# A one-core kernel of three nested Strassen levels: third level for three more pairs of steps, and the first loads on two queues

## The chip, the cores and the metric

The kernel runs on one core of one Trainium2 chip. The metric is the device time of one execution in microseconds. The core has the engines TensorE (PE, with its weight loads shown apart as PEld), VectorE (DVE), ScalarE (ACT), GpSimd (POOL) and SyncE (SP). SP computes nothing here; it issues most of the DMAs, and ACT and POOL issue the rest, each in the order of its own program.

## The reference

Two layers with residuals, all in f32, on x of 32 x 128 x 2048:

```python
x = x + ffn0(cond0(x))      # layer 0
x = x + ffn1(cond1(x))      # layer 1

# cond0: a mixture of 8 kernels of 128 x 128, weighted by an attention of the condition
att = softmax(gelu(gelu(emb @ W0 + b0) @ W1 + b1) @ W2 + b2)
out = einsum('boi,bih->boh', einsum('bk,koi->boi', att, weight), x) + (att @ bias_k)[:, :, None]

# ffn0: a dense layer 2048 -> 2048 with 16 low-rank updates of rank 16 (A, Bf)
out = einsum('bsd,od->bso', x, W) + bias
upd = einsum('ebsr,eor,e->bso', einsum('bsd,erd->ebsr', x, A), Bf, coeffs * scales)

# cond1: a grouped convolution of 9 taps along the 2048 (4 groups), plus ctx(cond) + bias
# ffn1: columns permuted, 16 heads of 128 -> 512 -> gelu -> 512 -> 128, columns permuted back
```

The kernel folds the low-rank updates into W (W plus scaled A times B^T), multiplies x by that W first, and applies the mixture afterwards, since both are linear.

## The kernel before, in words

**The large product.** x times W is a 2 x 2 block product by Strassen's scheme with seven products, in Winograd's form with its shared sums, at two levels. The outer level gives the seven rounds P1, P2, P6, P7, P5, P3, P4 (in this order). A round has eight steps g = 0 to 7, one for each group of four batch rows, so there are 56 steps. Each step is an inner scheme of seven products of 128 x 512 matmuls, four of them per product (`multiply`, line 342 for the DVE additions and L349 for the matmuls). f32 matmuls appear twice in the trace, so a step has 56 of them.

**The third level.** Where `in_pair(r, g)` holds, the steps g and g + 1 form a pair (`multiply_third`). Inner products P2 and P4 are left out of both steps (L439 shows the other five), and the pair makes them together in the odd step by a third scheme of seven quarter products of half-width matmuls (L450, additions L458). It needs `sq`, four sums over the pair's x tiles (`third_inputs`, L417 to L420, on POOL, but on DVE in round P6 and for g = 0), and two tiles of quarter weights (`third_weights`, L393 to L396 on POOL for the first, four operations on DVE, L1108, for the second). The partial results of the even step (`olds`) are held until the odd step has ended, and both are stored then (L277). `THIRD` names the rounds, and `SKIP` three pairs that are taken out.

**What surrounds a step.** SP loads the next step's x (L268) and the partial results (L273). POOL makes x's outer sums (L283) and inner sums (L311 to L314) in `x_combine`. At steps 2 to 6 the next round's outer weights are loaded (L507) and combined (L283), and at the end of a round `inner_weights` makes their inner sums (L252 to L256). DVE also makes the mixed kernels of `cond0` (L546) in steps 1 to 6 of most rounds.

**Slots.** All large tiles, of 8 KB per partition, share one pool of `SLOTS` = 25. A tile that is written first by a load or an operation waits in its engine's queue until a slot has been given back. Nothing behind it on that queue goes past it. The order of the instructions is the order of the source (`manual_schedule`), so it is written by hand throughout.

**The start.** After two warm-up matmuls on zeros (L157), A and B^T are loaded in pieces, A is scaled with `wsc` (L145), and for the first four W blocks `w_make` multiplies A by B^T (L180) and adds W (L184). W comes by L164. The other twelve blocks are made two at a time by a Strassen scheme (`w_make_two`, L223 and L226) ahead of the steps of round P1. Its sums of B^T (L211) are made between the additions of the fourth W block.

**The small chain.** `small()` computes the attention, the context of the convolution, the row indices and the convolution's weights. It is a generator, advanced once after each of the first six steps and twice after later ones, so a `yield` puts what follows behind another step's work.

**The last round and the rest.** In round P4 the kernel mixes (`mix_*`, L567 to L589) and convolves (`conv_*`) beside the steps, in stages of a third of a step. The permuted FFN (L818, L829, gathers L802, results L836) follows and takes the last 1100 us or so. `between(j)` is called after product j of a step and holds what is interleaved there.

Of the kernel before, what the change touches and what calls it, by code (L numbers as in the profile page):

```python
# [11 lines left out]
ALU = mybir.AluOpType  # L12
# [7 lines left out]
QW = 512  # L20
# [28 lines left out]


THIRD = ("P2", "P6", "P7", "P5", "P3")
SKIP = (("P2", 3), ("P6", 3), ("P5", 3))


@with_exitstack
def adaln_ffn_kernel(
# [16 lines left out]
    nc = tc.nc  # L73
# [53 lines left out]
    cs = const.tile([P, 4], FP, name="cs", tag="cs")  # L127
# [3 lines left out]
    a_sb = [slot(f"a_sb{h}", (P, 2, 2, 4, P)) for h in range(2)]  # L131
    bf_sb = [slot(f"bf_sb{h}", (P, 2, 2, QW)) for h in range(2)]

    def a_load(h, k0, k1):
        for ki in range(2):
            i0 = (2 * h + ki) * QW
            nc.sync.dma_start(
                a_sb[h][:, :, ki, k0:k1].rearrange("p c k i -> p c (k i)"),
                A[:, :, i0 + k0 * P : i0 + k1 * P],
            )  # L140
# [3 lines left out]
            cols = a_sb[h][:, c, :, k0:k1]  # L144
            nc.vector.tensor_scalar(cols, cols, wsc[:, c : c + 1], None, ALU.mult)  # L145

    def b_load(h, q, o0=0, n=QW):
        i0 = (2 * h + q) * QW + o0
        nc.sync.dma_start(bf_sb[h][:, :, q, o0 : o0 + n], BfT[:, :, i0 : i0 + n])

    def warm_up():

# [9 lines left out]
    def w_load(kh, oh, kc):  # L162
        t = slot(f"w_{kh}{oh}{kc}", (P, 2, 2, QW))
        nc.sync.dma_start(t.rearrange("p k o c -> p (k o c)"), WT[kh, oh, kc])  # L164
        return t
# [100 lines left out]
    def x_load(g, tp, kh):  # L266
        t = slot(f"xt_{g}{tp}{kh}", (P, 2, 2, QW))
        nc.sync.dma_start(t.rearrange("p k s c -> p (k s c)"), xT[g, tp, kh])  # L268
        return t
# [110 lines left out]
    def third_weights(name, rhs):  # L380


        ops, quarters = [], []
        for i, k in enumerate(("P2", "P4")):
            t = slot(f"{name}_q{i}", (P, 4, 2, NQ))
            q = {"P1": [], "P2": [], "P3": [], "P4": [], "P5": [], "P6": [], "P7": []}
            for kc in range(2):
                (r11, r12), (r21, r22) = (halves(rhs[k][2 * h + kc]) for h in range(2))
                for n, r in zip(q, (r11, r21, r22, t[:, 3, kc], t[:, 0, kc], t[:, 1, kc], t[:, 2, kc])):
                    q[n].append(r)  # L390
                if i == 0:
                    tt = nc.gpsimd.tensor_tensor
                    tt(t[:, 0, kc], r12, r11, ALU.subtract)  # L393
                    tt(t[:, 1, kc], r22, t[:, 0, kc], ALU.subtract)
                    tt(t[:, 2, kc], r22, r12, ALU.subtract)
                    tt(t[:, 3, kc], r21, t[:, 1, kc], ALU.subtract)  # L396
            quarters.append(q)
        (r11, r12), (r21, r22) = (
            [rhs["t4"][:, 2 * h : 2 * h + 2, n * NQ : (n + 1) * NQ] for n in range(2)]
            for h in range(2)  # L400
        )
        ops = [
            (t[:, 0], r12, r11), (t[:, 1], r22, t[:, 0]), (t[:, 2], r22, r12), (t[:, 3], r21, t[:, 1])
        ]
        return quarters, ops
# [452 lines left out]
    def small():  # L858
# [53 lines left out]
        for k in range(1, KEXP):  # L912
            nc.vector.scalar_tensor_tensor(
                aggb, ab[:, :, k], bk[:, k : k + 1], aggb, ALU.mult, ALU.add
            )

        for r in range(GR):
            p4 = bank()
            nc.tensor.matmul(
                p4[:, :B], lhsT=cw[:, r * P : (r + 1) * P], rhs=cond_s, start=True, stop=True  # L920
            )
            nc.vector.tensor_scalar(ctxb[:, r], p4[:, :B], fb[:, r : r + 1], None, ALU.add)
            done(p4)
        nc.vector.tensor_scalar(ctx34, ctxb, 0.75, None, ALU.mult)

        nc.vector.tensor_scalar(row, pos, 3, 9, ALU.bitwise_and, ALU.logical_shift_left)
        nc.vector.tensor_scalar(
# [62 lines left out]
    blocks = [  # L990
        (kh, oh, kc) for kh, oh in ((0, 0), (0, 1), (1, 1), (1, 0)) for kc in range(4)
    ]
    steps = [(r, g) for r in ROUNDS for g in range(NG)]
    warm_up()
    nc.sync.dma_start(cs, coeffs)
    nc.vector.tensor_tensor(wsc, cs[:, 0:2], cs[:, 2:4], ALU.mult)
    a_load(0, 0, 1)
    a_scale(0, 0, 1)
    b_load(0, 0, 0, QW // 2)
    b_load(0, 0, QW // 2, QW // 2)  # L1000
    b_load(0, 1)
    a_load(0, 1, 4)
    a_scale(0, 1, 4)
    wt = {k: w_load(*k) for k in blocks[0:2]}
    xs = {0: [x_load(0, 0, 0)]}
    for k in blocks[2:4]:
        wt[k] = w_load(*k)
    for q in range(2):
        b_load(1, q)
    for k in blocks[4:6]:  # L1010
        wt[k] = w_load(*k)
    nc.gpsimd.memset(wsum, 0.0)
# [26 lines left out]
    def olds_load(i):  # L1039
        r, g = steps[i]  # L1040
        olds[i] = [old and part_load(old, g) for old, _ in ADDED[r]]

    for i, (r, g) in enumerate(steps):
        ri = i // NG
        last_round = ri + 1 == len(ROUNDS)
        if i + 1 < len(steps):
            if i + 1 not in xs:
                xs[i + 1] = x_loads(*steps[i + 1])
            if not last_round:
                lhs[i + 1] = x_combine(*steps[i + 1], xs.pop(i + 1))  # L1050
                if r in THIRD and g == 0:
                    quarters, quarter_ops = third_weights(r, rhs)
# [42 lines left out]
        k0 = 3 * (g - NG)  # L1095
# [3 lines left out]
        def between(j):  # L1099
# [18 lines left out]
            if last_round:  # L1118
                if j == 3 and i + 1 < len(steps):
                    lhs[i + 1] = x_combine(*steps[i + 1], xs.pop(i + 1))  # L1120
                    olds_load(i + 1)
                if j in (2, 4):
                    stage(k0 + j // 2, stage_first)
                if j % 2:
                    stage_third(k0 + j // 2)
                else:
                    stage(k0 + j // 2, stage_second)
# [23 lines left out]
    for k, (g, h) in enumerate(heads):  # L1151
# [5 lines left out]
        t = ts.pop(k)  # L1157
# [75 lines left out]
```

## Time and profile before

| | us |
|---|---|
| median of 3 runs (lowest to highest) | 2597.11 (2597.05 to 2597.59) |
| the profiled execution | 2597.05 |
| its span in the profile | 2595.3 |
| PE busy in it | 2582.3 (99%) |
| POOL busy | 1321.1 (51%) |
| DVE busy | 1474.6 (57%) |
| ACT busy | 532.9 (21%) |

All times in what follows are microseconds from the start of the span. A line of the timeline gives the start and the length of a group of like instructions, the engine, the source line, the operation, the tile written <- the tiles read, the shape, the count, and in brackets the idle time of that engine just before and what ended it. A line of the windows gives the stretch, its length, and for PE, PEld, DVE, ACT and POOL the busy time and the number of instructions, then PE's granted clock, the DMA share and GB/s. An engine with q, as SPq, is the queue that issues DMAs. From 7.00 us to 36.00 us and from 1500 to 2580 us PE is busy in every window.

### The profile page before, as it was taken

The page shows a single profiled execution, that of the slowest core. Times are in us where ns is not written, and L with a number is a line of the kernel's source. Part 1 is how long each engine was busy: PE and PEld are TensorE (multiplying, and loading weights), DVE is VectorE, ACT ScalarE, POOL GpSimd, SP SyncE. Part 2 cuts the span into 40 slices and gives each one's busy share as a digit, 9 for nine tenths or more (in the row PEclk, how much of TensorE's full clock was granted, in tenths as well). Part 3 has the DMA queues.
Part 4 walks back from the last instruction along what each step waited for, and adds up shares of the span by engine and source line. Part 5 has one row for each costly group of instructions (what it writes and reads, how often), then busy time and mean ns, then how long its engine had stood idle before and what let it go on. Part 6 is the DMA issues. An engine that isn't in the chain of part 4 may idle for free. (4 is left out here: it accounts for less than half of the span.)

```text
span 2595.3 us, 21368 instructions
## 1 busy us (share of the span) xinstructions
PE 2582.3 (99%) x6876; PEld 1306.1 (50%) x6876; DVE 1474.6 (57%) x2326; ACT 532.9 (21%) x1099; POOL 1321.1 (51%) x1092
## 2 busy tenths in 40 slices
PE   9999999999999999999999999999999999999999
PEld 4444455455455555555444544555545554555543
DVE  5554465366455676554276666666666666666601
ACT  0000000000000000000011244444344444444432
POOL 7321657888976854967323234343444334434222
PEclk9999999999999999999999999999999999999999
DMA  7542458778457477474768788877777877787532
GB/s 311 221 161 98 185 194 335 303 310 331 192 227 303 178 315 300 195 308 167 246 213 267 229 301 266 257 231 228 228 231 240 257 225 223 230 257 229 163 128 89
DMA packets 188160, 608.28 MB, mean 234 GB/s; under 512 B 17680, under 2 KB 92944, under 8 KB 144016
## 3 DMA queue, kind: packets, MB, share of 16 engines
q1 hardware_dynamic: 149936, 473.74, 50.9%
q0 software_dynamic: 32704, 130.04, 14.9%
q10 hardware_dynamic: 5408, 3.13, 0.4%
q8 instruction: 55, 0.90, 0.1%
q14 instruction: 57, 0.47, 0.1%
HBM read 372.45 MB, written 200.84 MB: 221 GB/s over the span
## 5 line engine op out<-in xcount | busy, mean ns | idle before, releaser
L818 PE MATMUL bank<-t,ws 128*128 128x512 f32 x1024 | 460.3, 592 | 0.0
L829 PE MATMUL bank<-gl,ws 128*128 128x512 f32 x1024 | 460.2, 592 | 0.0
L836 POOL DMA_INDIRECT out<-t,orow x128 | 151.6, 1185 | 547.0 <-DVE t L834 480.4
L821 ACT ACTIVATE gl<-bank 128x512 f32<-128x512 f32 x512 | 306.3, 598 | 432.7 <-PE bank L818 426.3
L829 PEld LDWEIGHTS bank<-gl,ws 128*128 128x128 f32 x1024 | 194.6, 190 | 233.0 <-issue 231.5
L818 PEld LDWEIGHTS bank<-t,ws 128*128 128x128 f32 x1024 | 194.6, 190 | 226.6 <-issue 223.9
L567 POOL TENSOR_TENSOR x<-x,fb 128x512 f32<-128x512 f32 x128 | 173.1, 1381 | 213.1 <-DMA x<-in_x 126.4
L834 DVE TENSOR_TENSOR t<-bank,t 128x512 f32<-128x512 f32 x128 | 88.5, 691 | 327.1 <-PE bank L829 317.0
L573 ACT ACTIVATE bank<-w,aggb 128x512 f32<-128x512 f32 x128 | 80.9, 684 | 870.9 <-DMA w<-w_d 853.5
L439 PE MATMUL bank<-P_t,s_P 128*128 128x512 f32 x544 | 241.8, 592 | 0.0
L435 DVE TENSOR_TENSOR u<-bank,u 128x512 f32<-128x512 f32 x168 | 110.7, 688 | 194.9 <-PE bank L439 180.7
L283 POOL TENSOR_TENSOR xt<-xt,xt 128x512 f32<-128x512 f32 x128 | 162.7, 1303 | 104.9 <-DMA xt<-in_xT 97.1
L311 POOL TENSOR_TENSOR s_P<-xt 128x512 f32<-128x512 f32 x56 | 74.3, 1326 | 252.0 <-DMA xt<-in_xT 207.4
L439 PE MATMUL bank<-wo_P,s_P 128*128 128x512 f32 x448 | 199.1, 592 | 0.0
L546 DVE SCALAR_TENSOR_TENSOR ags<-mix,att_bc,ags 128x128 f32<-128x128 f32 x224 | 186.8, 834 | 4.7
L802 POOL DMA_INDIRECT t<-hx_d,row x128 | 131.6, 1028 | 61.7 <-issue 25.5
L439 PEld LDWEIGHTS bank<-P_t,s_P 128*128 128x128 f32 x544 | 103.4, 190 | 115.6 <-issue 112.6
L349 PE MATMUL bank<-P_t,s_P 128*128 128x512 f32 x352 | 154.7, 592 | 0.0
L439 PEld LDWEIGHTS bank<-wo_P,s_P 128*128 128x128 f32 x448 | 85.1, 190 | 95.2 <-issue 91.8
L674 PE MATMUL bank<-va,tw_l 128*128 128x256 f32 x512 | 121.2, 379 | 0.3 <-DVE va L658 0.3
L342 DVE TENSOR_TENSOR u<-bank,u 128x512 f32<-128x512 f32 x84 | 56.3, 685 | 112.7 <-PE bank L349 112.4
L674 PEld LDWEIGHTS bank<-va,tw_l 128*128 128x128 f32 x512 | 97.1, 190 | 41.2 <-issue 31.0
(188 smaller groups left out, 3589.9 us busy)
## 6 DMA issues: line engine op xcount, KB each, us to landing
xt<-in_xT SPq DMA_DIRECT2D x88, 1024.0 KB
u<-u_d SPq DMA_DIRECT2D x40, 1024.0 KB
wo_P<-wb_d SPq DMA_DIRECT2D x36, 1024.0 KB
u<-c_d SPq DMA_DIRECT2D x64, 512.0 KB
x<-in_x SPq DMA_DIRECT2D x32, 1024.0 KB
xg<-x SPq DMA_DIRECT2D x256, 128.0 KB
hx_d<-x1t SPq DMA_DIRECT2D x32, 1024.0 KB
hx_d<-ht SPq DMA_DIRECT2D x32, 1024.0 KB
```

The lines of the kernel that those rows point to most:

```text
L283: nc.gpsimd.tensor_tensor(out[:, i, j], a[:, i, j], b[:, i, j], op)
L349: nc.tensor.matmul(ps, lhsT=lhs[k][:, bass.ts(kc, P)], rhs=rhs[k][kc], start=first and kc == 0, stop=last and kc == 3, skip_group_check=True,)
L435: nc.vector.tensor_tensor(acc[:, si, oi], ps, acc[:, si, oi], ALU.add)
L439: nc.tensor.matmul(ps, lhsT=lhs[k][:, bass.ts(kc, P)], rhs=rhs[k][kc], start=first and kc == 0, stop=last and kc == 3, skip_group_check=True,)
L546: nc.vector.scalar_tensor_tensor(ag, mix[:, k], att, ag, ALU.mult, ALU.add)
L567: nc.gpsimd.tensor_tensor(xt[:, f], xt[:, f], late["fb"][:, f], ALU.add)
L674: nc.tensor.matmul(out, lhsT=w[:, 2 * i + r], rhs=rhs, start=first and r == 0, stop=last and r == 1, skip_group_check=True,)
L802: nc.gpsimd.indirect_dma_start(out=t.rearrange("p k t -> p (k t)"), out_offset=None, in_=hx_d[g].rearrange("l k t -> l (k t)"), in_offset= ...
L818: nc.tensor.matmul(pu, lhsT=w[:, m * P : (m + 1) * P], rhs=t[:, 0], start=True, stop=True)
L821: nc.scalar.activation(gl[m], pu, AF.Gelu)
L829: nc.tensor.matmul(pd, lhsT=w[:, (MC + m) * P : (MC + m + 1) * P], rhs=gl[m], start=(m == 0), stop=(m == MC - 1),)
L836: nc.gpsimd.indirect_dma_start(out=out, out_offset=bass.IndirectOffsetOnAxis(ap=orow[:, g, h : h + 1], axis=0), in_=t[:, 1], in_offset=None,)
```

## The change

- `SKIP` becomes empty: the last pairs (g = 6 and 7) of rounds P2, P6 and P5 run at the third level too.
- `third_weights`: for the first quarter tile, the operations that write parts 2 and 3 (L395, L396) are issued after those that write parts 0 and 1 (L393, L394) of both blocks.
- The first loads: `coeffs`, the second part of A's first block, the second half of B^T's first part and the rest of A go to ACT's queue. The rest stays on SP's.
- B^T's other half (`b_load(1, q)`) is issued ahead of W's third block, and the first x after W's third block.
- `small()` has two more `yield`s, around the context products.
- In the last round the x of step i + 2 is loaded after product 4 of step i, where it was loaded at the top of step i + 1.

```diff
--- before.py
+++ after.py
@@ -49,7 +49,7 @@
 
 
 THIRD = ("P2", "P6", "P7", "P5", "P3")
-SKIP = (("P2", 3), ("P6", 3), ("P5", 3))
+SKIP = ()
 
 
 @with_exitstack
@@ -131,10 +131,10 @@
     a_sb = [slot(f"a_sb{h}", (P, 2, 2, 4, P)) for h in range(2)]
     bf_sb = [slot(f"bf_sb{h}", (P, 2, 2, QW)) for h in range(2)]
 
-    def a_load(h, k0, k1):
-        for ki in range(2):
+    def a_load(h, k0, k1, engs=(nc.sync, nc.sync)):
+        for ki, eng in enumerate(engs):
             i0 = (2 * h + ki) * QW
-            nc.sync.dma_start(
+            eng.dma_start(
                 a_sb[h][:, :, ki, k0:k1].rearrange("p c k i -> p c (k i)"),
                 A[:, :, i0 + k0 * P : i0 + k1 * P],
             )
@@ -144,9 +144,9 @@
             cols = a_sb[h][:, c, :, k0:k1]
             nc.vector.tensor_scalar(cols, cols, wsc[:, c : c + 1], None, ALU.mult)
 
-    def b_load(h, q, o0=0, n=QW):
+    def b_load(h, q, o0=0, n=QW, eng=nc.sync):
         i0 = (2 * h + q) * QW + o0
-        nc.sync.dma_start(bf_sb[h][:, :, q, o0 : o0 + n], BfT[:, :, i0 : i0 + n])
+        eng.dma_start(bf_sb[h][:, :, q, o0 : o0 + n], BfT[:, :, i0 : i0 + n])
 
     def warm_up():
 
@@ -380,7 +380,7 @@
     def third_weights(name, rhs):
 
 
-        ops, quarters = [], []
+        others, quarters = [], []
         for i, k in enumerate(("P2", "P4")):
             t = slot(f"{name}_q{i}", (P, 4, 2, NQ))
             q = {"P1": [], "P2": [], "P3": [], "P4": [], "P5": [], "P6": [], "P7": []}
@@ -392,9 +392,11 @@
                     tt = nc.gpsimd.tensor_tensor
                     tt(t[:, 0, kc], r12, r11, ALU.subtract)
                     tt(t[:, 1, kc], r22, t[:, 0, kc], ALU.subtract)
-                    tt(t[:, 2, kc], r22, r12, ALU.subtract)
-                    tt(t[:, 3, kc], r21, t[:, 1, kc], ALU.subtract)
+                    others.append((t[:, 2, kc], r22, r12))
+                    others.append((t[:, 3, kc], r21, t[:, 1, kc]))
             quarters.append(q)
+        for op in others:
+            nc.gpsimd.tensor_tensor(*op, ALU.subtract)
         (r11, r12), (r21, r22) = (
             [rhs["t4"][:, 2 * h : 2 * h + 2, n * NQ : (n + 1) * NQ] for n in range(2)]
             for h in range(2)
@@ -914,6 +916,7 @@
                 aggb, ab[:, :, k], bk[:, k : k + 1], aggb, ALU.mult, ALU.add
             )
 
+        yield
         for r in range(GR):
             p4 = bank()
             nc.tensor.matmul(
@@ -922,6 +925,7 @@
             nc.vector.tensor_scalar(ctxb[:, r], p4[:, :B], fb[:, r : r + 1], None, ALU.add)
             done(p4)
         nc.vector.tensor_scalar(ctx34, ctxb, 0.75, None, ALU.mult)
+        yield
 
         nc.vector.tensor_scalar(row, pos, 3, 9, ALU.bitwise_and, ALU.logical_shift_left)
         nc.vector.tensor_scalar(
@@ -992,21 +996,21 @@
     ]
     steps = [(r, g) for r in ROUNDS for g in range(NG)]
     warm_up()
-    nc.sync.dma_start(cs, coeffs)
+    nc.scalar.dma_start(cs, coeffs)
     nc.vector.tensor_tensor(wsc, cs[:, 0:2], cs[:, 2:4], ALU.mult)
-    a_load(0, 0, 1)
+    a_load(0, 0, 1, (nc.sync, nc.scalar))
     a_scale(0, 0, 1)
     b_load(0, 0, 0, QW // 2)
-    b_load(0, 0, QW // 2, QW // 2)
+    b_load(0, 0, QW // 2, QW // 2, nc.scalar)
     b_load(0, 1)
-    a_load(0, 1, 4)
+    a_load(0, 1, 4, (nc.scalar, nc.scalar))
     a_scale(0, 1, 4)
     wt = {k: w_load(*k) for k in blocks[0:2]}
-    xs = {0: [x_load(0, 0, 0)]}
-    for k in blocks[2:4]:
-        wt[k] = w_load(*k)
     for q in range(2):
         b_load(1, q)
+    wt[blocks[2]] = w_load(*blocks[2])
+    xs = {0: [x_load(0, 0, 0)]}
+    wt[blocks[3]] = w_load(*blocks[3])
     for k in blocks[4:6]:
         wt[k] = w_load(*k)
     nc.gpsimd.memset(wsum, 0.0)
@@ -1119,6 +1123,8 @@
                 if j == 3 and i + 1 < len(steps):
                     lhs[i + 1] = x_combine(*steps[i + 1], xs.pop(i + 1))
                     olds_load(i + 1)
+                if j == 4 and i + 2 < len(steps):
+                    xs[i + 2] = x_loads(*steps[i + 2])
                 if j in (2, 4):
                     stage(k0 + j // 2, stage_first)
                 if j % 2:
```

## The prediction

> **What bounds the kernel now.** I read the page's busy shares first, then what TensorE (PE) waits for, then windows cut at the starts of steps, then the timeline of the engines that feed PE.
>
> ```profile
> span 2595.3 us, 21368 instructions
> PE 2582.3 (99%) x6876; PEld 1306.1 (50%) x6876; DVE 1474.6 (57%) x2326; ACT 532.9 (21%) x1099; POOL 1321.1 (51%) x1092
> ```
>
> PE is idle for 2595.3 - 2582.3 = 13.0 us. About 6 of them are the tail (from 2580 us on it is busy 9.03 of 15.3 us), which the change leaves alone. So time can come only from fewer PE instructions, or from these waits (total, times, longest):
>
> ```profile
> PE bank L223 <- DVE w L226: 2.4, 3, 1.7
> PE bank L157 <- DVE warm L154: 1.5, 1, 1.5
> PE bank L180 <- DMA bf_sb<-in_BfT: 1.0, 1, 1.0
> PE bank L349 <- DVE u L342: 0.9, 1, 0.9
> ```
>
> Next, windows of one pair of steps each (length, then busy time and instructions by engine): P2's third pair, P2's last, P7's last, P5's last.
>
> ```profile
> 399.25:445.67 46.42, 46.42 (x138) 25.84 (x137) 25.78 (x35) 0.00 (x0) 39.27 (x33) 1.00 0.82 331
> 445.67:493.73 48.06, 48.06 (x113) 21.28 (x112) 12.65 (x23) 0.00 (x0) 31.99 (x28) 1.00 0.68 264
> 820.32:866.74 46.42, 46.42 (x138) 25.84 (x136) 16.84 (x27) 0.00 (x0) 27.65 (x23) 1.00 0.53 205
> 1006.65:1054.72 48.07, 48.07 (x114) 21.28 (x113) 21.61 (x38) 0.00 (x0) 26.14 (x21) 1.00 0.65 256
> ```
>
> A third-level pair takes 46.42 us (136 weight loads, 56 of them for half-width matmuls), an ordinary one 48.06 (112 full ones), PE busy throughout in both. P7's last pair already has the third level and a full 25-slot pool around it, and PE does not wait.
>
> **Third level for three more pairs.** PE: 48.06 - 46.42 = 1.64 us each, 3 x 1.64 = **4.92 us**, if nothing new is late. What it adds elsewhere: five more accumulations on DVE per pair at 0.69 us (3.4 us, twice that in P5 with two accumulators), and four operations for sq. DVE is busy 12.65 of 48.06 and 21.61 of 48.07 us in the P2 and P5 pairs; P5's earlier pair is busy 33.15 of 46.42 with PE fully fed, so DVE is cover enough. If that cover were gone, each late us would be one on PE, since the banks come back through DVE.
>
> In P2 and P5 sq is made on POOL (4 x 1.3 = 5.2 us), in P6 on DVE at the end of the even step. Queued behind P2's sq on POOL is the combine of P6's last weight block, then x_combine for P6. Here are POOL's rows from P2 into P6, and then PE's (start, length, then the work):
>
> ```profile
> 461.90 9.83 POOL L283 TENSOR_TENSOR xt<-xt,xt 128x512 f32<-128x512 f32 x8 [14.75 <-DMA xt<-in_xT]
> ...
> 498.21 11.19 POOL L283 TENSOR_TENSOR xt<-xt,xt 128x512 f32<-128x512 f32 x8
> ...
> 519.86 0.77 POOL L393 TENSOR_TENSOR P_q<-wo_P 128x256 f32<-128x256 f32 x1
> 520.72 0.73 POOL L394 TENSOR_TENSOR P_q<-wo_P,P_q 128x256 f32<-128x256 f32 x1
> ```
> ```profile
> 521.22 1.03 PE L450 MATMUL bank<-P_q,sq 128*128 128x256 f32 x4
> ```
>
> POOL waits 14.75 us for P6's x, so the 5.2 us of sq are hidden; without that wait they would cost 5.2. From 461.90 to 522.9 POOL never rests. That x load was issued at 448.1, behind the stores of the pair before, so this chain does not move when PE gets 1.64 us ahead. The tight place is PE's first use of the second L394 result: its weights load 0.43 us after 521.22, at 521.65, and the result is there at 521.45. A lead of 1.64 us alone would make PE wait 1.4. The reordering of the weight sums answers that: L395 and L396 (0.68 pitch each) go behind both blocks' L393 and L394, so the second L394 ends 1.36 us earlier, at 520.1, against a need at 520.0. I charge 0.2 us. At the other two round changes the same L394 has more room: P7's ends at 699.7 for a need at about 709, P3's at 1075.0 for one at 1082.6. There the lead is free.
>
> Stores: the even step's C tiles stay until the odd step ends, so SP, no longer held by their store in mid pair, runs ahead to the next loads and can only stop for a slot. Counting tiles late in P2's pair: 7 weights, 2 quarters, 4 next weights, 2 X, 1 s, 1 sq, 3 C, next X and s, 3 inner sums: 25 of 25, and three x tiles of P6's second step on top. P7's last pair counts 7+2+4+2+1+1+3+2+2+3 = 27 and shows PE busy 46.42 of 46.42; P6 counts 27, P5 29. Tiles come back within the odd step (X of the even step after the second quarter product, t1 after P5, t2 after P6), before POOL's inner sums ask. Bounds: 0 (as P7) and the rival's price below; I take 0, the row of the same kind.
>
> **The start.** cs and half of the first A tile move to ACT's queue. Rows of before:
>
> ```profile
> 0.74 1.28 ACT L344 ACT_TABLE_LOAD   x1 [0.74 <-PEq L1219]
> ...
> 2.56 1.92 SPq L149 DMA_DIRECT2D bf_sb<-in_BfT  x3
> ...
> 4.59 0.62 DVE L145 TENSOR_SCALAR a_sb<-a_sb,wsc 128x256 f32<-128x256 f32 x2 [2.01 <-DMA a_sb<-in_A]
> ...
> 6.21 9.99 PE L180 MATMUL bank<-bf_sb,a_sb 128*128 128x256 f32 x26 [0.97 <-DMA bf_sb<-in_BfT]
> ```
>
> PE's first real matmul waits for B^T's first half, SP's fourth issue. It becomes the second: it no longer stands behind cs (0.45 us) and one A part (0.66), so it lands 1.1 us earlier, at about 5.1 us, where the warm-up ends anyway (four at a pitch of 0.85 us from 4.18: 5.03). If ACT does its table load first, cs goes out 1.28 us later, the scaled A is ready at about 5.9, and only 0.3 us are won; if transfers of both queues also slow each other, nothing, or 0.3 lost. On the other side, PE runs its first nine 256-column matmuls at 0.43 us and the next ones at 0.22: the step in clock comes at 10.18, after 3.97 us of work without a gap. (The window's granted clock says 1.00 there, so only the pitch shows it.) If the step stays at 10.18, 1.1 us more at half pace is worth 0.55; if it moves with the first matmul, 1.1; and if no real matmul ran at half pace any more, 1.1 + 9 x 0.21 = 3.0. Bounds -0.3 and 3.0; I take **1.0**, nearest to the row that moves with its load.
>
> [...]
>
> B^T's other half stands behind two W blocks and one x block that it will pass: 3 MB, about 7 us at the 420 GB/s which the windows show from 10 to 50 us. DVE waited for it until 33.51 (1.98 us) while evacuating W's fourth block, and PE paid the 1.68 us in the waits above (L223 on L226). With it there, DVE's four sums (1.15 each) fit between the evacuations at the banks' pitch of 1.72 (0.69 + 1.15 less overlap: 1.68 seen). So **1.7 us**. W's fourth block and x are later by 1 and 2 MB (2.5 and 5 us); x is combined at 32.1 with POOL never waiting for it, and W's fourth block is wanted at 30.8. I estimate its landing at 29 to 30; a late us there would take from the 1.7.
>
> **The small chain.** The ctx products leave the place before the last two-block W product: DVE's L922 to L934 stood before L226 there (222.74 to 224.97), and PE waited 0.28 and 0.60. They now follow in the next step, where no W product follows. **0.9 us**; not below zero, as the instructions stay the same. Everything after it in the chain is a step later: its tw and t1 tiles hold two slots a step longer in P2. PE has 24 us of lead there, so nothing.
>
> **The last round** loads x a third of a step sooner, at the price of a slot and before SP's conv stores. POOL waits for x (13.50 us at 1393) without PE waiting; PE's waits there total 1.2 us (0.87 and 0.30). Bounds: 1.2 won, 2 lost (two such waits more); I take 0.
>
> **Sum**: 4.92 - 0.2 + 1.0 + 1.7 + 0.9 = 8.3 us. The profiled execution took 2597.05 us (span 2595.3 and 1.75 around it), the median of the runs is 2597.11. 2597.1 - 8.3 = **2588.8 us**.
>
> **Rivals.** (1) Slots decide, and it ends slower. If P6's second x load waits for the end of P2's pair (492.1, not 471.8), it lands 13.8 us later (448.1 to 461.9 is such a load), at 506, and L394 ends about 22 us after, at 528, 8 us late. In P7 the load at 677.8 would land at 691.6, L394 end 14.6 later at 706.2, needed at 705.7; in P3 1049.8 + 14.2 + 15.2 = 1079.2, needed at 1077.7: 10 us in all. And if P6's sq on DVE waits for a slot, every evacuation queues behind it: up to an even step, 17.17 us; half is 8.6. Together about 19: 2608. It decides from 8.3 + 5.2 = 13.5 us of waits. For it: 25 to 29 tiles in 25 slots. Against it: P7's last pair. 0.12.
> (2) The third level gives nothing: POOL's chains do not move, and PE waits out its lead at each round change. 8.3 - 4.7 = 3.6, so 2593.5. For it: the 0.2 us of room at 521. Against it: 8 to 9 us of room at the other two. With partial slot waits, 0.14.
> (3) The first loads bring nothing and W's fourth block comes late: 8.3 - 1.0 - 1.0 = 6.3, so 2590.8, still faster; it is in the forecast's chance, 0.74.
>
> 0.2% (5.2 us) is what a measurement of this kernel can tell from no change: faster 0.74, same 0.14, slower 0.12. The range goes from 2585.5 (clock step early, no waits in the last round) to 2597, which leaves out the slow rival and part of rival 2. The forecast's own range is 2586 to 2591.9.
>
> **What would show it.** The three windows at 46.4 us with PE fully busy; PE's second quarter product in P6 waiting under 0.5 us for L394; no DMA wait at L211 and no L226 wait before L223; first L180 matmul at 5 to 5.6 us. Wrong if PE shows waits on POOL or DVE at the starts of P6, P7 or P3, or if DVE stands at L417 waiting for a slot.

## The result, and the profile after

| | before | after |
|---|---|---|
| median of 15 runs each | 2597.59 | 2603.13 |
| lowest to highest | 2596.68 to 2599.70 | 2601.07 to 2604.82 |
| the profiled execution (its span) | 2597.05 (2595.3) | 2604.82 (2603.0) |

The changed kernel takes 1.002 times as long (95% interval 1.0013 to 1.0027): 5.5 us slower, where 8.3 us faster was forecast. Its profiled execution is the slowest of the fifteen, so the two profiles lie further apart (7.8 us) than the medians do.

Line numbers below are those of the changed kernel: L441 is the matmul that was L439, L437 and L460 the additions that were L435 and L458, L452 the quarter matmul (L450), L1112 the second quarter tile on DVE (L1108), L676 and L660 a matmul and a DVE operation behind the last round (L674 and L658). The variants of the experiments have numbers of their own.

The page after, the line of busy times first:

```profile
span 2603.0 us, 21554 instructions
PE 2580.5 (99%) x6948; PEld 1320.7 (51%) x6948; DVE 1491.6 (57%) x2350; ACT 532.3 (20%) x1099; POOL 1333.9 (51%) x1100
```

PE is busy 1.8 us less, and its idle time has grown from 13.0 to 22.5 us. The list of what PE waited for names nearly all of the growth (total, times, longest):

```profile
PE bank L441 <- DVE p L437: 9.2, 1, 9.2
PE bank L180 <- DMA bf_sb<-in_BfT: 3.6, 2, 1.9
PE bank L157 <- DVE warm L154: 1.5, 1, 1.5
PE bank L676 <- DVE va L660: 1.1, 3, 0.7
...
PE bank L223 <- DVE w L226: 0.2, 1, 0.2
```

A wait that before did not have at all stands at the top: 9.2 us, once. The L223 wait that the moved load of B^T was to remove is down from 2.4 to 0.2, but the wait at L180 has gone from 1.0 to 3.6. Next the three pairs that were given the third level, P2's, P6's and P5's last, as windows between the starts of their steps:

```profile
446.57:492.99 46.42, 46.42 (x138) 25.84 (x136) 17.04 (x27) 0.00 (x0) 35.98 (x31) 1.00 0.75 273
643.67:690.09 46.42, 46.42 (x137) 25.84 (x136) 26.45 (x31) 0.00 (x0) 43.82 (x35) 1.00 0.62 242
1015.68:1062.10 46.42, 46.42 (x137) 25.84 (x136) 26.67 (x46) 0.00 (x0) 22.28 (x19) 1.00 0.66 259
```

46.42 us three times with PE full, as the prediction had it: 4.9 us are won. They are lost in the step after the first of them, P6's first:

```profile
492.99:521.58 28.59, 19.43 (x41) 8.31 (x40) 8.02 (x10) 0.00 (x0) 27.88 (x25) 0.82 0.40 152
```

This step took 17.17 us before, with PE full and the clock at 1.00, and takes 28.59:

```profile
493.73:510.90 17.17, 17.17 (x42) 7.60 (x40) 8.13 (x9) 0.00 (x0) 16.85 (x14) 1.00 0.91 363
```

PE's granted clock is 0.82 in it now. DVE's first write of P6's second quarter tile in the kernel before came straight after the addition ahead of it, without a wait:

```profile
497.98 0.83 DVE L1108 TENSOR_TENSOR P_q<-P_t 128x512 f32<-128x512 f32 x1
```

The timeline of the changed kernel in that stretch, from three engines:

```profile
496.62 0.69 DVE L437 TENSOR_TENSOR p<-bank,p 128x512 f32<-128x512 f32 x1 [2.15 <-PE bank L441]
...
501.44 9.80 POOL L283 TENSOR_TENSOR xt<-xt,xt 128x512 f32<-128x512 f32 x8
511.27 0.69 DVE L1112 TENSOR_TENSOR P_q<-P_t 128x512 f32<-128x512 f32 x1 [13.95 <-POOL xt L283]
...
512.62 9.13 PE L441 MATMUL bank<-wo_P,s_P 128*128 128x512 f32 x16 [9.16 <-DVE p L437]
```

Read it from the bottom up. PE waits 9.16 us for a bank that DVE's addition L437 must empty. DVE does not come to it, because in its queue ahead stands L1112, the first write of P6's second quarter tile `P_q`. What ends DVE's 13.95 us of waiting is POOL's L283, the outer sum of the second step's x, which neither writes `P_q` nor reads it. A wait on work that has no data in common points to a wait for a slot: the quarter tile would get the slot of an x tile, when POOL has read it for the last time. The experiments test that. After the wait, PE's first matmuls of 512 columns start at distances (pitches) of 1.02, three times 0.85 and 0.67 us, with 0.43 for the later ones: about 2.1 us more. This slow stretch is called half pace below. Together this step loses 11.4 us.

By steps, from the starts in both traces: the start +1.8, the small chain -1.25, P2's second step +0.4, the three pairs 3 x -1.65, P6's first step +11.4, the last round and the part after it +0.4; the sum is 7.8, the difference of the two spans.

The start is the other part of the story. PE's and DVE's lines from 4 to 19 us:

```profile
6.93 1.10 PE L180 MATMUL bank<-bf_sb,a_sb 128*128 128x256 f32 x4 [1.91 <-DMA bf_sb<-in_BfT]
9.75 8.82 PE L180 MATMUL bank<-bf_sb,a_sb 128*128 128x256 f32 x20 [1.72 <-DMA bf_sb<-in_BfT]
18.11 1.15 DVE L145 TENSOR_SCALAR a_sb<-a_sb,wsc 128x768 f32<-128x768 f32 x2 [13.42 <-DMA a_sb<-in_A]
```

The first matmul comes 0.7 us later than before (6.21), where 1.1 earlier was expected, the second piece of B^T makes a second wait, and the rest of A is scaled at 18.11 in place of 13.62. The clock adds to it: the four matmuls after the first wait stand at pitches of 0.29, 0.22 and 0.22 us, those after the second at 0.59 and then 0.43 until 14.9 us, where before had 0.22 from 10.18 on. Being late by then, PE waits only 0.2 us for the rest of A; in the other five profiles with this start it waits 0.5 to 3.4. The DMA view of 7 to 14 us shows why the rest of A is late, by queue (packets, MB, share of the engines), q1 being SP's and q10 ACT's:

```profile
q1 hardware_dynamic: 372, 2.18, 75.2%
q10 hardware_dynamic: 402, 0.57, 25.9%
```

The two queues move about as many packets as each other, but a packet of ACT's queue has 0.57 MB / 402 = 1.4 KB on average, one of SP's, with W and x in it, 5.9 KB. Packet for packet, the queue that carries the rest of A gets a fifth of the bytes (0.57 of 2.75 MB), and W and x, which nobody needs yet, get most of the others. Together the queues moved 393 GB/s there and one queue 303 before: more bytes, in a worse order. The rate is not the second queue's merit: e14 below, where SP's queue carries all but 0.02 MB in this window, moved 392 GB/s. What the second queue changed is what landed first: the rest of A was scaled 4.5 us later. Why the first matmul itself is 0.7 us later was not followed up.

### The profile page after: what moved, and what is told of

It reads as the page before. It is cut to its first block, busy times and chain, and to the rows that moved or that the text cites. A ratio compares the mean times of both kernels' runs of the same rounds, so it can differ in the third digit from the quotient of the medians.

```text
span 2603.0 us, 21554 instructions
## 1 busy us (share of the span) xinstructions
PE 2580.5 (99%) x6948; PEld 1320.7 (51%) x6948; DVE 1491.6 (57%) x2350; ACT 532.3 (20%) x1099; POOL 1333.9 (51%) x1100
## 5 line engine op out<-in xcount | busy, mean ns | idle before, releaser
L441 PE MATMUL bank<-P_t,s_P 128*128 128x512 f32 x640 | 284.4, 592 | 0.0
L437 DVE TENSOR_TENSOR u<-bank,u 128x512 f32<-128x512 f32 x192 | 125.9, 687 | 212.1 <-PE bank L441 196.9
L441 PE MATMUL bank<-wo_P,s_P 128*128 128x512 f32 x512 | 229.7, 597 | 9.2 <-DVE p L437 9.2
L283 POOL TENSOR_TENSOR xt<-xt,xt 128x512 f32<-128x512 f32 x128 | 163.8, 1311 | 104.7 <-DMA xt<-in_xT 89.4
L441 PEld LDWEIGHTS bank<-P_t,s_P 128*128 128x128 f32 x640 | 121.6, 190 | 136.0 <-issue 132.5
L548 DVE SCALAR_TENSOR_TENSOR ags<-mix,att_bc,ags 128x128 f32<-128x128 f32 x224 | 179.5, 801 | 4.7
L441 PEld LDWEIGHTS bank<-wo_P,s_P 128*128 128x128 f32 x512 | 98.0, 192 | 119.5 <-issue 107.4
L437 DVE TENSOR_TENSOR p<-bank,p 128x512 f32<-128x512 f32 x96 | 64.7, 688 | 141.4 <-PE bank L441 134.8
L676 PE MATMUL bank<-va,tw_l 128*128 128x256 f32 x512 | 121.9, 380 | 1.1 <-DVE va L660 1.1
L676 PEld LDWEIGHTS bank<-va,tw_l 128*128 128x128 f32 x512 | 96.9, 190 | 42.9 <-issue 32.1
L587 DVE TENSOR_TENSOR x<-bank,x 128x512 f32<-128x512 f32 x128 | 87.7, 690 | 50.7 <-PE bank L584 21.3
```

The source lines that it names most:

```text
L283: nc.gpsimd.tensor_tensor(out[:, i, j], a[:, i, j], b[:, i, j], op)
L437: nc.vector.tensor_tensor(acc[:, si, oi], ps, acc[:, si, oi], ALU.add)
L441: nc.tensor.matmul(ps, lhsT=lhs[k][:, bass.ts(kc, P)], rhs=rhs[k][kc], start=first and kc == 0, stop=last and kc == 3, skip_group_check=True,)
L548: nc.vector.scalar_tensor_tensor(ag, mix[:, k], att, ag, ALU.mult, ALU.add)
L676: nc.tensor.matmul(out, lhsT=w[:, 2 * i + r], rhs=rhs, start=first and r == 0, stop=last and r == 1, skip_group_check=True,)
```

## The experiments

**The theories.** A: the third level in P2's last pair leaves too few slots, P6's second quarter tile waits for one, and everything else is small. B: the wait at P6 comes from the other parts, or is not what costs the time. C: the new start costs or earns a good part of the difference. D: the earlier load of x in the last round does. From e6 on, where the slot wait is gone, theory A in an expectation is what the runs until then had shown, and stands against the rival named there.

All times in the table are medians with the ratio to the kernel before on the same chip and its 95% interval.

| run | median | ratio | first product of P1 at | P6's first step waits |
|---|---|---|---|---|
| changed kernel | 2603.13 | 1.0013 to 1.0027 | 51.50 | 9.2 |
| e1, P2's pair left out | 2596.02 | 0.9984 to 1.0002 | 52.24 | 0 |
| e2, quarter tile kept | 2594.10 | 0.9978 to 0.9996 | 50.08 | 0 |
| e3, first loads on SP | 2601.38 | 1.0006 to 1.0024 | 49.29 | 8.4 |
| e4, x not earlier | 2603.92 | 1.0013 to 1.0033 | 50.18 | 7.3 |
| e5, third level alone | 2603.13 | 1.0012 to 1.0031 | 49.61 | 7.9 |
| e6, kept, old start | 2593.96 | 0.9977 to 0.9995 | 49.58 | 0 |
| e7, kept, old sums | 2598.53 | 0.9990 to 1.0008 | 50.33 | 0 |
| e8, kept, loads on SP | 2593.33 | 0.9974 to 0.9992 | 49.10 | 0 |
| e9, sums on DVE, loads on SP | 2600.57 | 1.0003 to 1.0021 | 49.41 | 0 |
| e10, sums on DVE, new start | 2600.43 | 1.0001 to 1.0019 | 51.52 | 0 |
| e11, sums on DVE, rest of A on SP | 2598.09 | 0.9992 to 1.0010 | 49.50 | 0 |
| e12, sums on DVE, old start | 2602.03 | 1.0003 to 1.0021 | 50.03 | 0 |
| e13, P6's sums on DVE, loads on SP | 2592.49 | 0.9971 to 0.9989 | 49.48 | 0 |
| e14, P6's sums on DVE, rest of A on SP | 2591.14 | 0.9962 to 0.9982 | 48.90 | 0 |

### The slot

**e1_skip_p2**

```diff
-SKIP = ()
+SKIP = (("P2", 3),)
```

> The changed kernel, but P2's last pair stays at two levels (SKIP holds P2's pair 3 alone). Theory A: what the change lost is one wait, DVE's first write of the second quarter tile (L1112) standing for a slot at P6's first step, with every evacuation behind it: 9.2 us of PE idle and 2.1 us at half pace after it. Without P2's third-level pair the wait is gone: 11.4 us back, 1.65 us of P2's gain lost, so about 2603.1 - 9.8 = 2593.3 us, and P6's and P5's last pairs still 46.4 us each. Rival B: the slots are short at each of the three pairs, and the wait shows up at P7's or P3's first step instead, 2600 us or more.

Measured 2596.02. PE has no wait at the starts of P6, P7 and P3, so the pairs of P6 and P5 bring no slot wait; P2's alone does. From P2's start to P7's, the profile is 9.8 us shorter than the changed kernel's, which is theory A's sum. The median is 2.7 above theory A's 2593.3, and under theory B's bound. The profile has part of that: 0.7 at the start (first product at 52.24, where the changed kernel had 51.50) and 1.1 behind the start of the last round, where the two kernels are the same.

**e2_q_kept**

```diff
+    kept = []
...
-            t = slot(f"{name}_q{i}", (P, 4, 2, NQ))
+            if i == 1 and kept:
+                t = kept[0]
+            else:
+                t = slot(f"{name}_q{i}", (P, 4, 2, NQ))
+                if i == 1:
+                    kept.append(t)
```

The second quarter tile gets its slot once, in P2, and is written again in every later round.

> The changed kernel, but the second quarter tile is one tile kept over all five rounds, so that DVE's write of it needs no new slot. Theory A: DVE no longer stands at L1112 in P6's first step, PE's 9.2 us wait and the 2.1 us at half pace go, all three pairs are worth 1.65 us: 2603.1 - 11.4 = 2591.7 us, with at most 1 us of waiting for L394 left. Rival B: POOL's x_combine for P6's second step, which ends at 511, is what PE needs, and the wait only moves from DVE to POOL: PE is idle 5 us or more in P6's first two steps, 2598 us or more.

Measured 2594.10: 9.0 us below the changed kernel, with all three pairs in, and 2.4 above theory A's sum. The timeline, DVE's line and then PE's (L459 is the quarter matmul here):

```profile
495.81 1.34 DVE L1119 TENSOR_TENSOR P_q<-P_t 128x512 f32<-128x512 f32 x1
```
```profile
520.88 3.29 PE L459 MATMUL bank<-P_q,sq 128*128 128x256 f32 x14 [0.78 <-POOL P_q L401]
```

The same operation (now L1119) runs at 495.81, straight after the addition before it, with no wait. Nothing about its data or about POOL's work was changed, only where the tile lies, so the wait was for the slot. What is left at P6's second step is the wait that the prediction had named, for POOL's second L394 (here L401): 0.99 us in two parts where 0.2 was charged, and the step is 1.5 us longer than in the kernel before.

**e5_third_alone** is the kernel before with only this:

```diff
-SKIP = (("P2", 3), ("P6", 3), ("P5", 3))
+SKIP = ()
```

> The kernel before with nothing but the third level switched on for the last pairs of P2, P6 and P5. Theory A (the third level by itself runs out of slots at P6's second step, because the two quarter tiles of P6 are taken while P2's last pair is in flight): the three pairs bring 3 x 1.65 = 4.9 us, and DVE's first write of P6's second quarter tile waits for POOL's combination of x, so that PE waits about 9 us at P6's second step and runs about 2 us more at half pace; in all 2597.7 - 4.9 + 11 = 2604, between 2602.5 and 2605.5. Theory B (the wait arises only together with the other parts, which move POOL's and the queues' work): no such wait, and 2597.7 - 4.9 = 2592.8, with 2594.3 if the old order of the sums costs the 1.5 us that the reorder is to save.

Measured 2603.13, in theory A's interval, with 7.85 us of wait and about 3 us of half pace after it (11.0 together). The third level makes the loss without help from any other part.

### The weight sums, and what bounds P6 next

**e7_q_kept_old_sums** is e2 with the old order:

```diff
-                    others.append((t[:, 2, kc], r22, r12))
-                    others.append((t[:, 3, kc], r21, t[:, 1, kc]))
+                    tt(t[:, 2, kc], r22, r12, ALU.subtract)
+                    tt(t[:, 3, kc], r21, t[:, 1, kc], ALU.subtract)
```

> The changed kernel with its second quarter tile kept over all rounds and the weight sums of the quarters in their old order (all four of the first half of the inner dimension, then all four of the second). With the new order PE waits 0.99 us for POOL's sums at P6's second step (0.21 for the first half, 0.78 for the second). Theory A: the second half's two sums come two operations of 0.73 us later, that wait grows by 1.5 us to 2.3 in all, and the time is 2594.1 + 1.5 = 2595.6; no other wait appears. Rival: the order of POOL's sums is covered by PE's work on the first half, the wait stays within 0.3 us of 0.99 and the time within 0.5 us of 2594.1.

Measured 2598.53: by the medians the reorder is worth 4.4 us here, three times what was expected, and by the step in the profiles 3.7. PE's timeline and the window of the step:

```profile
520.23 0.67 PE L459 MATMUL bank<-P_q,sq 128*128 128x256 f32 x2 [0.77 <-POOL P_q L401]
523.17 4.97 PE L459 MATMUL bank<-P_q,sq 128*128 128x256 f32 x14 [2.27 <-POOL P_q L401]
```
```profile
508.98:543.46 34.48, 31.44 (x97) 19.22 (x96) 21.03 (x25) 0.00 (x0) 33.06 (x32) 0.95 0.84 337
```

The second wait grew by the expected 1.5 us (0.78 to 2.27), and the first by 0.6. But the 14 matmuls behind it took 4.97 us in place of 3.29, and the granted clock of the step is 0.95: 3.0 us of idle time in 3.7 us put PE back to half pace. In e8, 1.35 + 0.79 us of the same two waits did not. Two gaps of 0.77 and 2.27 us were enough in e7, so going from 1.0 to 3.0 us of waiting cost 3.7 us in the profile and not 2.0.

**e6_q_kept_start_old** and **e8_q_kept_start_sp** are e2 with other starts. e6 has the start of before; e8 has

```diff
-    nc.scalar.dma_start(cs, coeffs)
+    nc.sync.dma_start(cs, coeffs)
...
-    a_load(0, 0, 1, (nc.sync, nc.scalar))
+    a_load(0, 0, 1)
...
-    b_load(0, 0, QW // 2, QW // 2, nc.scalar)
+    b_load(0, 0, QW // 2, QW // 2)
...
-    a_load(0, 1, 4, (nc.scalar, nc.scalar))
+    a_load(0, 1, 4)
```

> The changed kernel with its second quarter tile kept over all rounds (no new slot for it at each round) and the whole start, its queues and the order of its loads, as in the kernel before. Theory A (the third level and the small chain earn, the new start earns nothing): first product at 49.7 us as before, pairs -4.95, small chain -1.25, about 1.9 us left to P6's second step and P2's second step (waits for POOL's sums and DVE), last round and what follows within 0.5: 2597.7 - 4.3 = 2593.4, at or below the 2594.1 of the same kernel with the new start. Theory C (the earlier half of B^T earns at least 1.5 us once the other parts are right): 2595 or more, above the kernel with the new order on one queue that runs beside it by 1.5 us or more.

> The changed kernel with its second quarter tile kept over all rounds and all first loads on SyncE's queue, in the new order (the other half of B^T ahead of the third block of W). Theory A (two queues cost what the order earns): first product at 49.3 us as in the run of the changed kernel with the first loads on one queue, so 0.4 us ahead of the old order and 0.9 to 2 us ahead of two queues: 2593.0, between 2592.2 and 2593.6, the fastest of these. Theory C (W's later fourth block takes back what B^T's place brings): not below the kernel with the old start, both at 2593.4 within 0.3 us.

Measured 2593.96 and 2593.33, both where theory A had them. They don't price the start, though. e2, e6 and e8 begin P6 at 491.57, 490.70 and 490.23, and its third step at 539.48, 539.23 and 539.29: a lead of 1.3 us is reduced to 0.2. In e6 and e8 PE waits 1.6 and 2.1 us there for POOL's L401, and POOL has no idle time over 0.5 us from 462.5 to 523. POOL's chain into P6 (x_combine, inner sums, weight sums) is what ends there, whoever comes early.

**e9 to e12** take four of POOL's weight sums out of that chain, in all rounds, each with another start. Common to them, against e2:

```diff
-                    tt = nc.gpsimd.tensor_tensor
-                    tt(t[:, 0, kc], r12, r11, ALU.subtract)
-                    tt(t[:, 1, kc], r22, t[:, 0, kc], ALU.subtract)
+                    firsts.append((t[:, 0, kc], r12, r11))
+                    firsts.append((t[:, 1, kc], r22, t[:, 0, kc]))
...
-                nc.vector.tensor_tensor(*quarter_ops.pop(0), ALU.subtract)
+                for op in quarter_ops.pop(0):
+                    nc.vector.tensor_tensor(*op, ALU.subtract)
```

`quarter_ops` now holds pairs, one of `firsts` and one of the second tile's operations; the first tile is kept over the rounds too, and POOL makes `others` after the round's first step.

> The changed kernel with all first loads on SyncE's queue in the new order, both quarter tiles kept over all rounds, and the first four sums of the first quarter tile (t0 and t1 of both halves of the inner dimension) moved from POOL, where they stood behind x_combine, to DVE in the four gaps of each round's first step; POOL keeps the four others. Theory A (at P6's second step POOL is the bound, so that what is earned ahead of it is lost there): PE's wait for POOL's sums, 2.1 us in the same kernel without the move, falls to 0.4 or less, P6's third step starts at 537.3 instead of 539.3, and the time is 2593.3 - 2.0 = 2591.3. Rival (DVE or x_combine is late next): at least 1.5 us of wait stays at P6's second step under another name, and the time is 2592.8 or more.

Measured 2600.57, 7.2 us worse than e8: a miss, and the rival's cause in another place. At P6 it did what it was for (47.93 us from P6's start to its third step, 49.06 in e8). But in P2 and P5, where POOL had been in time, DVE is now late. PE's timeline there (L453 is the quarter matmul, L461 its additions):

```profile
334.40 3.72 PE L453 MATMUL bank<-P_q,sq 128*128 128x256 f32 x16 [1.89 <-DVE p L461]
```
```profile
896.69 5.41 PE L453 MATMUL bank<-P_q,sq 128*128 128x256 f32 x16 [3.46 <-DVE u L461]
```

DVE's additions stand behind sq and the added sums: 1.89 us of wait in P2, 3.46 in P5, and after the longer one 5.41 us for what takes 3.72 after the shorter: half pace again. The length of the wait alone doesn't decide that. In e12's profile, the same place in P2 has a wait as long as e9's, and half pace after it:

```profile
335.01 5.41 PE L453 MATMUL bank<-P_q,sq 128*128 128x256 f32 x16 [1.88 <-DVE p L461]
```

What else decides is not shown.

**e13_p6_dve_start_sp** moves the sums in P6 alone:

```diff
+                    if name == "P6":
+                        firsts.extend(two)
+                    else:
+                        for op in two:
+                            nc.gpsimd.tensor_tensor(*op, ALU.subtract)
```

> Both quarter tiles kept, all first loads on SyncE's queue in the new order, and the four sums moved from POOL to DVE in round P6 alone, so that P2 and P5 go as in the kernel without the move (2593.3). Theory A (POOL bounds P6's second step, DVE comes 1.25 us late next, as it did with the sums moved in all rounds): from the start of P6 to its third step 47.9 us in place of 49.1, no waits at P2's and P5's second steps, 2593.3 - 1.1 = 2592.2. Rival (what is earned at P6 is given back later, since the POOL work behind it stays): P7's start within 0.3 us of the 678.6 of the kernel without the move, and 2593.0 or more.

Measured 2592.49, 0.8 below e8, which the medians alone could not tell from nothing; the profiles show where some of it comes from: P6's third step comes after 48.2 us and P7 starts 0.5 us sooner. PE now waits 1.5 us for DVE there, where it waited 2.1 for POOL. So POOL was the bound at P6 and DVE stands close behind it, which limits what this is worth.

### The start and the last round

**e3_start_sp** is the changed kernel with the edit of e8.

> The changed kernel, but all first loads are on SP's queue again; B^T's other half stays ahead of W's third block. Theory A: the second queue is what made the start late, since packets of both queues alternate and the 1 and 1.5 KB packets of A and B^T wait for W's 8 KB packets; the first real matmul is back at about 6.2 us, A's rest at 13.6, and the 1.8 us that B^T's place wins are kept: the first step's first product at 47.9 us instead of 51.5, 2603.1 - 3.6 = 2599.5 us. Rival C: the order of the blocks made the start late; then the first product stays later than 49.7 us and the time at 2602 us or more.

Measured 2601.38, between the theories. The first product comes at 49.29, 0.4 ahead of before and not the 1.8 that were expected of B^T's place. DVE's timeline has the reason:

```profile
32.12 0.69 DVE L184 TENSOR_TENSOR w<-bank,w 128x512 f32<-128x512 f32 x1 [3.33 <-DMA w<-in_WT]
```

W's fourth block, pushed back by B^T's 1 MB, lands at 32.1; the prediction had estimated 29 to 30 against a need at 30.8. DVE's wait for B^T is gone and one for W is there in its place, so PE's wait for DVE at L223 is 2.2 us here, where before had 2.4.

**e10_q_dve**, **e11_q_dve_rest_sp** and **e12_q_dve_start_old** put the other starts on e9. e10 has the change's start. e11 has it with one line back:

```diff
-    a_load(0, 1, 4, (nc.scalar, nc.scalar))
+    a_load(0, 1, 4)
```

> As the run with the sums on DVE, but with the change's start: first loads on both queues. Here nothing at P6 hides the start. Theory A (packets of the two queues alternate, and the queue of small packets falls behind): first product between 50.0 and 52.3 us as in the other runs with this start, 0.9 to 3 us after the one-queue start's 49.1 to 49.3, and the time above that of the one-queue start by as much: 2592.2 to 2594.3. Rival (the start differs in the profiles by chance only): time within 0.5 us of the one-queue start.

> As the run with the sums on DVE and the change's start, but the rest of A goes back to SyncE's queue; the coefficients, one half of A's first piece and the second half of B^T's first piece stay on ScalarE's. Theory A (what costs is that the rest of A, in 1.5 KB packets, shares the engines with the 8 KB packets of W): the rest of A is scaled by 13.5 us and not at 18, PE doesn't wait for it, first product at 49.3 or before, 2591.3 or less. Rival (the first pieces on two queues cost as well): PE's waits for B^T's pieces stay at 3 us or more together, first product at 50 us or later, 2592 or more.

> As the run with the sums on DVE and all first loads on SyncE's queue, but with the order of the blocks as in the kernel before (B^T's other half after W's fourth block). Theory A (the new order earns 0.4 to 0.6 us, as the first products at 49.1 to 49.3 against 49.6 to 49.7 say, because W's fourth block comes later for it): 0.5 us above the run with the new order, 2591.8. Rival (the new order earns the 1.7 us of the wait that it removes): 1.5 us or more above.

The medians (2600.43, 2598.09 and 2602.03, beside e9's 2600.57) don't order the starts, and all lie 6 to 10 us above what was expected, as e9 does, since DVE is late in P2 and P5 in each: e10's profile has its first product 2.1 us after e9's, and its median is the same. The intervals are about 2.3 us wide on each side, so differences of this size were out of reach; the clock adds to the scatter (e12's profile has half pace after P2's wait too, 5.41 us for what took 3.72 in e9). What orders them is the first product over all profiles with the same start: 49.6 to 50.0 with the start of before (four), 49.1 to 49.5 with the new order on SP (four), 50.1 to 52.2 with the change's start (six). The three groups do not overlap, if only by 0.05 and 0.1 us, with one profile to a kernel. So B^T's place earns about 0.4 us at the first product and the second queue costs 0.6 to 3.1 against the same order on one, and varies from run to run. With the rest of A back on SP it is 49.50 here.

**e14_p6_dve_rest_sp** is e13 with e11's start.

> As the run with the sums moved in P6 alone, with the start in which only the coefficients, half of A's first piece and the second half of B^T's first piece are on ScalarE's queue. Theory A (only the rest of A in the second queue costs): first product at 49.5 us again, within 0.4 of the one-queue start, and 2592.3, within 0.5 of the run beside it. Rival (the two small pieces on the second queue cost a good part of the 1.7 us too): first product at 50.0 or later and 0.7 us or more above the run beside it.

Measured 2591.14, the lowest of all and 0.28% below the kernel before (0.18 to 0.38). Against e13 the 1.35 us are within the uncertainty. Its first product is at 48.90, and the lines of its start are:

```profile
6.83 1.10 PE L180 MATMUL bank<-bf_sb,a_sb 128*128 128x256 f32 x4 [1.70 <-DMA bf_sb<-in_BfT]
8.68 15.50 PE L180 MATMUL bank<-bf_sb,a_sb 128*128 128x256 f32 x38 [0.74 <-DMA bf_sb<-in_BfT]
11.20 1.15 DVE L145 TENSOR_SCALAR a_sb<-a_sb,wsc 128x768 f32<-128x768 f32 x2 [6.61 <-DMA a_sb<-in_A]
```

The rest of A is scaled at 11.20, where the change had 18.11 and before 13.62; PE still waits twice for B^T's pieces (2.4 us), so the two small pieces on the second queue do not help the first matmul. What hurt was the rest of A on that queue: both kernels that put it back (e11 and this one) have their first product at 49.5 or before.

**e4_no_early_x** takes the last round's new load out:

```diff
-                if j == 4 and i + 2 < len(steps):
-                    xs[i + 2] = x_loads(*steps[i + 2])
```

> The changed kernel without the earlier x load in the last round. Theory A: the load's place is worth little: P4 loses the 0.9 us that it won (PE's wait for DVE at its sixth step returns), and the 1.2 us of waits on DVE (L660) in the FFN part go, so 2603.1 us within 0.6. Rival D: the earlier load takes slots and SP's place from the convolution, and without it the time is 2 us or more lower.

Measured 2603.92, so theory D falls. PE's wait of 0.9 us at L349 for DVE is back, as in before; from the last round's start to the end the two profiles lie within 0.3 us of each other. That part scatters by more: the thirteen profiles with the earlier load stand at -0.5 to +1.5 us against before, and e5, which has the old load, at +2.4.

## Why the prediction was wrong, step by step

**Stores: the step that failed.** "Counting tiles late in P2's pair ... 25 of 25, and three x tiles of P6's second step on top", with P7's last pair as the row of the same kind and a bound of 0 taken. The count went on to the x tiles of P6's second step, but left out P6's two quarter tiles, which are first written in P6's first step, the second of them by DVE ahead of its own additions. P7's last pair, counted alike, had 27 tiles and no wait, but what follows it differs: P5 loads two x tiles a step, P6 three. That this difference is what saves P7 was not tried; that P2's pair is the one that overflows, and by this tile, is shown by e1, e2 and e5. Measured: 11.4 us in place of 0.

**Rival 1** had the mechanism, with 0.12: slots decide, and a DVE operation that waits for a slot holds up all evacuations. It named sq at L417 and the x loads; it was the quarter tile at L1108, which the prediction had not put in any count. Its half even step, 8.6 us, is close to the 9.16 measured, but by luck: it was half of an upper bound, for another tile; the late loads of P7 and P3, 10 us in its sum of 19, did not happen. Its threshold of 13.5 us for a slower kernel also failed: 11.4 was enough, as the other terms brought less.

**Third level, 4.92:** right, three times 1.65 (46.42 us windows).

**The weight sums, -0.2:** right in kind. Without the slot wait, 0.99 us of waiting were left (e2), and more the earlier PE arrived (2.1 in e8), since POOL's chain does not move. Rival 2 said that of all round changes; it holds for P6's alone, as no wait appears at P7's and P3's. The 1.4 us for the old order came out as 3.7 in e7's step (4.4 by the medians), 1.7 of it because the clock fell.

**The start, 1.0 (bounds -0.3 to 3.0):** wrong sign. First products of 50.1 to 52.2 with the change's start against 49.1 to 49.5 with the same order on one queue: -0.6 to -3.1, outside the bounds. In the profile of the changed kernel the first L180 matmul came at 6.93 and not at 5.1, and a second wait for B^T followed. The bound below had only the table load and "0.3 lost" for queues that slow each other. No run shows that 0.3; what the runs showed in its place is 402 packets of 1.4 KB on ACT's queue beside 372 of 5.9 KB on SP's from 7 to 14 us, and the rest of A scaled 4.5 us later.

**B^T's other half, 1.7:** 0.4 on one queue (e3, e8, e9, e13). DVE's wait for B^T went as said, but PE's wait at L223 stayed at 1.1 to 2.2 us in these four; the term that was mis-sized is W's landing, 32 us and not 29 to 30. Why it lands that late was not followed up.

**The small chain, 0.9:** 1.25, with e6 against e5 as the cleanest pair (their offset to before is the same at the first product within 0.04, and 1.3 us apart by P1's eighth step).

**The last round, 0:** nothing against it: the profile after lies 0.4 above before in that part and e4 0.6, both inside its scatter.

## What to carry to other kernels

Count a shared pool's tiles through the first step after the edit's last one, and for each tile ask which engine makes its first write and what queues behind that write; a precedent counts only if its successor is the same too. Lengthening tile lifetimes by one step cost 11.4 us here, where the work it removed was worth 4.9, and a tile that is rewritten every round can simply keep its slot (e2, 9.0 us below the changed kernel). A second DMA queue is a choice of order: with the rest of A on ACT's queue, which moved 0.57 MB in 7 us beside SP's 2.18 with W and x in it, that rest was scaled at 18.11 us, where it was at 13.62 in the kernel before and at 11.20 with that load back on SP's queue (e14). And price a wait with what it does to PE's clock: the 1.88 us in e12 were followed by 1.69 us of lost pace, the 1.89 in e9 by none.

## What the runs showed of the hardware

- Half pace came back after waits of 9.16 us (changed kernel: 9.13 us for 16 matmuls that take 7.03 ahead of the wait), 7.85 (e5: 9.98 for 16 such) and 3.46 us (e9: 5.41 for what takes 3.72), after 0.77 + 2.27 us with only two matmuls between them (e7: 4.97 in place of 3.29), and after 1.88 us in e12 (5.41 in place of 3.72). It did not after 1.89 us at the same place in e9 (3.72), 1.35 + 0.79 (e8: 3.29), 1.50 (e13: 3.72) or 1.85 us (e14: 3.72). So waits near 1.9 us went either way. Where it came back, these lines are 1.7 to 2.95 us longer. e3 and e4, with waits of 8.4 and 7.3 us, have a granted clock of 0.997 over the whole execution, as the changed kernel has; e2 has 1.000.
- In the kernel before, the first nine L180 matmuls stand 0.43 us apart (the first two 0.56) after 3.78 us of warm-up and a gap of 0.97 us. After 3.97 us without a gap, from 10.18 to 11.75 us, they stand 0.22 us apart (the first two 0.27).
- With two queues busy in the changed kernel, each moved about the same number of packets: from 7 to 14 us SP's 372 and ACT's 402, with 2.18 and 0.57 MB, and from 3 to 7 us 460 and 456, with 0.61 and 0.35 MB.
